# Two-layer transformer block on one core: three of the four GpSimd steps of a ternary weight piece move one slot each in the written order

## The chip, the cores and the metric

The kernel runs on one core of one Trainium2 chip. The core has a matrix engine (TensorE, PE in the profile), a vector engine (VectorE, DVE), a scalar engine (ScalarE, ACT), GpSimd (POOL) and a queue engine for transfers (SyncE, SP). Each engine has an instruction queue of its own, and the program ties the queues together by semaphores. The metric is the device time of one execution in microseconds (us); smaller is better. The runs of the kernel before took 1178.61, 1179.34 and 1179.58 us, median 1179.34 us.

## The reference

Two layers, each an attention and a feed-forward network on the same normalised input, added to the residual. What matters here is the attention of layer 0 (2 x 1024 tokens, 32 query heads of width 8, causal) and the weights of layer 1's feed-forward network, which the reference quantises to three values per group of 64 before it uses them:

```python
def ternary_quant(w_fp32, g=GROUP_SIZE):
    w = w_fp32.astype(jnp.bfloat16)
    w_g = w.reshape(-1, g)
    scale = jnp.clip(jnp.mean(jnp.abs(w_g), axis=-1, keepdims=True), 1e-08, None)
    q = jnp.clip(jnp.round(w_g / scale), -1, 1)
    w_hat = (q * scale).reshape(w.shape)
    return w + jax.lax.stop_gradient(w_hat - w)

x = x + _L0_attn_ref(xn, ...) + _L0_ffn_ref(xn, ...)
xn = _layernorm(x, axis=-1)
x = x + _L1_attn_ref(xn, ...) + _L1_ffn_ref(xn, ...)
```

The last line of `ternary_quant` is computed as it stands, (q * scale - w) + w in bfloat16, so a piece of weights ends in four elementwise steps: the sign from two comparisons, times the scale, minus w, plus w.

## The kernel before

**Layer 0's attention** (`attention0`) works in blocks of 128 queries, sixteen of them: the eight of batch 0 upwards, then the eight of batch 1 downwards. Two streams run side by side in it. One finds each row's largest score: `max_unit` has TensorE make scores in PSUM (L930 the causal mask, L958 the products) and VectorE reduce each 128x512 tile of them (L970); the score tiles come from a pool of three PSUM buffers, so TensorE can't run far ahead of VectorE. `take_max` closes a block's maxima, and they go through memory into the rows of the query tile. The other stream weighs: `weigh` makes transposed scores (L1022), ScalarE takes the exponentials (L1032), and where the key block is the query block itself (j == i) GpSimd clears what lies above the diagonal in each of them (the `affine_select`, L1036; called a select here). `gather` multiplies with the values (L1052), one key block later.

**The written order.** The text of the program is a chain of slots. `one_slot` writes some maxima (`advance`), then at most one piece of layer 0's feed-forward network (`pieces`, with its bfloat16 elementwise work on VectorE, L196 to L206 and L295 to L305, and `out_piece`, whose additions into the residual, L261, are on GpSimd), then calls `tick`. `tick` counts the slot and runs what `after(n, f)` had set down n slots before. Behind each `one_slot`, the main loop writes one `weigh`: two exponentials, and in a diagonal block two selects. So the four selects of a half block are written in two consecutive slots.

Only TensorE's queue is held to the written order (`manual_schedule(engines={PE})`). The queues of the other engines are laid out by the framework's planner when the program is built: it goes through a simulated time, and gives an engine that is free the earliest written instruction among those that are ready. `tc.issue_after(ins)` adds one condition: what the block writes for the engine of `ins` is queued behind `ins`. Here `ins` is `reduced`, the latest L970, so this holds VectorE's instructions and no others.

**The ternary weights** are made during layer 0 in twelve pieces of 128x512: eight of `w_gate_up`, into `wgu_bf`, four of `w_proj`, into `wp`, for use in layer 1. `ternary` is a generator. Its first step loads the piece by a DMA from GpSimd's queue (L326, two buffers `tw`), its second takes absolute values on VectorE (L329), and its third has TensorE sum the groups (L332), VectorE scale and compare (L334, L336, L337) and GpSimd do the four last steps, L338 to L341, each of which reads what the one before it wrote. They are called the four links here. `next_weights` is called when a block's maxima are done, from the fourth block on: it does the second step of one piece, sets `rest_of_weights` down for two slots later, and takes the first step (the load) of the next piece. `rest_of_weights` takes the third step. Nothing in layer 0 reads the finished weights: `wgu_bf` is first read behind the attention, when it is copied to float32 (L1294), `wp` by L667.

## Time and profile before

| what | number |
|---|---|
| median of three runs | 1179.34 us |
| the profiled execution | 1180.16 us, its span 1178.4 us |
| mean granted TensorE clock over the span | 0.936 |
| busy over the span | PE 88%, DVE 65%, ACT 46%, POOL 29% |
| busy from 90 to 790 us (layer 0's attention) | PE 607.89, DVE 571.12, ACT 428.42, POOL 244.05 us |
| one link on POOL (L338 to L341), 48 of them | 1.14 to 1.71 us |
| one select on POOL (L1036), 128 of them | 637 ns median |
| start of the twelve pieces' first link | 177.3, 225.0, 277.8, 352.5, 416.7, 480.3, 543.6, 602.1, 651.2, 687.0, 717.5, 736.4 us |

The profile is of one execution. [...] A timeline row gives start, length, engine, line and operation, the tiles written and read, and in brackets how long the engine had been idle before and whose result it waited for. The chain of waits is followed back from the last instruction to what released each step. TensorE's matmul ends are modelled.

### The profile page before, as it was taken

The page shows a single profiled execution, that of the slowest core. Times are in us where ns is not written, and L with a number is a line of the kernel's source. Part 1 is how long each engine was busy: PE and PEld are TensorE (multiplying, and loading weights), DVE is VectorE, ACT ScalarE, POOL GpSimd, SP SyncE. Part 2 cuts the span into 40 slices and gives each one's busy share as a digit, 9 for nine tenths or more (in the row PEclk, how much of TensorE's full clock was granted, in tenths as well). Part 3 has the DMA queues.
Part 4 walks back from the last instruction along what each step waited for, and adds up shares of the span by engine and source line. Part 5 has one row for each costly group of instructions (what it writes and reads, how often), then busy time and mean ns, then how long its engine had stood idle before and what let it go on. Part 6 is the DMA issues. An engine that isn't in the chain of part 4 may idle for free.

```text
span 1178.4 us, 19285 instructions
## 1 busy us (share of the span) xinstructions
PE 1039.2 (88%) x7446; PEld 497.8 (42%) x7462; DVE 764.8 (65%) x1448; ACT 545.2 (46%) x983; POOL 345.4 (29%) x394
## 2 busy tenths in 40 slices
PE   5758787897988989897989998989999999999998
PEld 2333331231432222232323333334566676676676
DVE  7467988889688997789896899334333433433331
ACT  2004461673456757586767777742232322322221
POOL 2007233324235121412223335564222312312200
PEclk9758896998899989998999999999899999999989
DMA  5342101101102010100000110019431431421200
GB/s 173 112 110 73 48 3 38 21 21 45 49 5 50 1 27 10 41 5 8 21 19 10 27 28 3 5 19 132 62 52 28 80 65 30 86 51 28 38 19 19
DMA packets 65859, 48.99 MB, mean 42 GB/s; under 512 B 20840, under 2 KB 59368, under 8 KB 65768
## 3 DMA queue, kind: packets, MB, share of 16 engines
q1 hardware_dynamic: 60568, 39.05, 15.4%
q0 software_dynamic: 4112, 8.26, 2.9%
q8 instruction: 58, 0.95, 0.3%
q10 hardware_dynamic: 1088, 0.46, 0.1%
q14 instruction: 33, 0.27, 0.1%
HBM read 34.12 MB, written 15.20 MB: 42 GB/s over the span
## 4 chain that ended last, share of the span: by engine, by line
PE 55%; DVE 27%; DMA 7%; ACT 4%; POOL 3%; issue 2%; SPq 1%; DVEq 0%; ACTq 0%; POOLq 0%
DVE mx L970 14%; PE f1gu L632 8%; PE acc L1052 8%; PE s L1022 6%; PE f1o L667 5%; PE m L958 3%; PE sk L524 3%; PE sq L489 3%; PE gu L288 2%; DMA qscr<-ptq 2%; PE pqk L440 2%; ACT p L1032 2%; PE m L930 1%; DMA qkv<-all 1%; SPq L882 1%
## 5 line engine op out<-in xcount | busy, mean ns | idle before, releaser
L970 DVE TENSOR_REDUCE mx<-m 128x1 f32<-128x512 f32 (+3 forms) x608 | 372.8, 654 | 91.4 <-PE m L958 55.2
L1032 ACT ACTIVATE p<-s 128x512 f32<-128x512 f32 x576 | 307.0, 604 | 133.7 <-PE s L1022 131.2
L1052 PE MATMUL acc<-p,v 128*9 128x512 f32 x1152 | 171.1, 613 | 2.4 <-ACT p L1032 1.2
L958 PE MATMUL m<-k,qmain 64*128 64x512 bf16 (+3 forms) x384 | 94.8, 357 | 50.5 <-DVE mx L970 39.2
L1036 POOL TENSOR_SCALAR_AFFINE_SELECT p<-p 128x512 f32<-128x512 f32 x128 | 84.8, 685 | 162.2 <-ACT p L1032 161.9
L632 PE MATMUL f1gu<-xnT,wgu 128*128 128x512 f32 x256 | 117.6, 603 | 3.1 <-DVE wgu L1294 3.1
L958 PE MATMUL m<-kmain,qmain 64*128 64x512 bf16 (+3 forms) x384 | 83.4, 333 | 24.9 <-DVE mx L970 23.0
L958 PEld LDWEIGHTS <-qmain 64*128 64x128 bf16 x768 | 50.3, 99 | 80.4 <-issue 51.2
L930 PEld LDWEIGHTS <-ident_h 64*128 64x128 bf16 x832 | 45.2, 97 | 88.1 <-issue 65.3
L646 POOL TENSOR_TENSOR sq<-h 128x512 f32<-128x512 f32 x28 | 29.2, 1041 | 180.0 <-DVE h L642 180.0
L930 PE MATMUL m<-mask_q,ident_h 64*128 64x128 bf16 (+3 forms) x832 | 75.2, 221 | 2.4 <-DVE mx L970 2.3
L1022 PE MATMUL s<-qmain,k 64*128 64x512 bf16 x288 | 67.8, 393 | 9.0 <-ACT ob L258 3.1
L632 PEld LDWEIGHTS f1gu<-xnT,wgu 128*128 128x128 f32 x256 | 47.5, 195 | 51.8 <-issue 47.8
L1022 PE MATMUL s<-qmain,kmain 64*128 64x512 bf16 x288 | 64.0, 389 | 4.9 <-ACT p L1032 2.3
L1022 PE MATMUL s<-qlast,k 35*128 35x512 bf16 x288 | 64.0, 390 | 0.0
L641 DVE SCALAR_TENSOR_TENSOR h<-h,f1gu 128x512 f32<-128x512 f32 x32 | 22.0, 687 | 64.5 <-ACT h L640 64.5
L1022 PEld LDWEIGHTS <-k 64*128 64x128 bf16 (+1 forms) x576 | 21.1, 95 | 97.9 <-issue 89.8
L497 DVE TENSOR_REDUCE m<-sq 128x16 f32<-128x2048 f32 x16 | 36.7, 2292 | 39.6 <-PE sq L489 38.9
L1022 PE MATMUL s<-qlast,klast 35*128 35x512 bf16 x288 | 61.1, 386 | 0.0
L667 PE MATMUL f1o<-k,h 128*128 128x256 f32 x256 | 59.4, 388 | 0.5 <-DVE on L557 0.5
L667 PEld LDWEIGHTS f1o<-k,h 128*128 128x128 f32 x256 | 48.9, 193 | 9.0 <-issue 1.7
L640 ACT ACTIVATE h<-f1gu 128x512 f32<-128x512 f32 x32 | 19.1, 597 | 65.7 <-PE f1gu L632 65.6
(274 smaller groups left out, 1597.6 us busy)
## 6 DMA issues: line engine op xcount, KB each, us to landing
qmain<-qscr SPq DMA_DIRECT2D x64, 96.0 KB
qkv<-all SPq DMA_DIRECT2D x16, 384.0 KB
qscr<-ptq POOLq DMA_DIRECT2D x6, 384.0 KB, 4.1
x<-in_x SPq DMA_DIRECT2D x16, 128.0 KB
qmain<-qscr SPq DMA_DIRECT2D x32, 64.0 KB
qs<-qkv SPq DMA_DIRECT2D x16, 128.0 KB
ks<-qkv SPq DMA_DIRECT2D x16, 128.0 KB
vs<-qkv SPq DMA_DIRECT2D x16, 128.0 KB
```

The lines of the kernel that those rows point to most:

```text
L489: nc.tensor.matmul(ps[:, s, r, :], columns(q, slice(S * s, S * s + HD + 8), 4 * b + r), columns(k, slice(S * s, S * s + HD + 8), 4 * b + r ...
L497: nc.vector.tensor_reduce(m, ps, AX.X, ALU.max, negate=True)
L524: nc.tensor.matmul(ps[:, s, r, :], columns(k, slice(S * s, S * s + HD + 9), 4 * b + r), columns(q, slice(S * s, S * s + HD + 9), 4 * b + r ...
L632: nc.tensor.matmul(ps[g], wgu[:, k, g * HID + hc * P : g * HID + (hc + 1) * P], xnT[n][:, k, :], start=(k == 0), stop=(k == 1),)
L667: nc.tensor.matmul(po, hs[hc // 2][:, hc % 2, i * P : (i + 1) * P], wp[:, hc, :], start=(hc == 0), stop=(hc == NHC - 1),)
L930: nc.tensor.matmul(out[e][:, :, lo:], ident_h[rows, t, :], rhs.to_broadcast([HALF, out[e].shape[1], P - lo]), start=start and t == 0, stop ...
L958: nc.tensor.matmul(sc[e][:, s * width : (s + 1) * width], qst[b, i][0][rows, p, :], kst[b][0][rows, lo // 512, p // 4, 0:width], start=not ...
L970: reduced = nc.vector.tensor_reduce(mx[b, i][:, part, e, pairs[0] : pairs[0] + n], sc[e][:, : n * width].rearrange("p (s k) -> p s k", s=n ...
L1022: nc.tensor.matmul(sc[e], kst[b][n][rows, j // 4, u, j % 4 * P : (j % 4 + 1) * P], qst[b, i][n][rows, 4 * u : 4 * u + 4, :], start=n == 0, ...
L1032: nc.scalar.activation(p, sc[e], AF.Exp, scale=scale)
L1036: nc.gpsimd.affine_select(out=by_head, in_=by_head, compare_op=ALU.is_ge, fill=0.0, base=0, pattern=[[0, 4], [1, P]], channel_multiplier=-1,)
L1052: nc.tensor.matmul(acc[32 * s : 32 * s + HD0 + 1, :], vst[b][:, j, 4 * G + s, :], ps[s], start=(j == 0), stop=(j == i),)
```

## The change

The four links are no longer written in one step of the generator: there is a `yield` behind each of the first three. `rest_of_weights` takes one step, and as long as the generator isn't exhausted it sets itself down again for the next slot. So the first link stays in the slot it was written in, and the second, third and fourth are written one, two and three slots later. 

```diff
         nc.gpsimd.tensor_tensor(m, m, lo, ALU.subtract)
+        yield
         nc.gpsimd.tensor_tensor(m, m, s, ALU.mult)
+        yield
         nc.gpsimd.tensor_tensor(m, m, w, ALU.subtract)
+        yield
         nc.gpsimd.tensor_tensor(dst, m, w, ALU.add)
...
             def rest_of_weights(u):
                 with tc.issue_after(reduced.ins):
-                    next(u, None)
+                    more = next(u, self_end)
+                if more is not self_end:
+                    after(1, lambda: rest_of_weights(u))
```

## The prediction

> **What bounds the kernel now.** I read the page first: busy shares, slices, then the chain that ended last.

> ```profile
> PE 1039.2 (88%) x7446; PEld 497.8 (42%) x7462; DVE 764.8 (65%) x1448; ACT 545.2 (46%) x983; POOL 345.4 (29%) x394
> ...
> POOL 2007233324235121412223335564222312312200
> ...
> PE 55%; DVE 27%; DMA 7%; ACT 4%; POOL 3%; issue 2%; SPq 1%; DVEq 0%; ACTq 0%; POOLq 0%
> ```

> GpSimd is busy 29% of the span and holds 3% of the chain. So the links' own duration (48 of about 1.2 us, some 57 us) isn't what ends late; they can only matter through whom they hold up. There are two candidates: the selects queued behind them, for which the value matmuls wait, and VectorE, which holds 27% of the chain.

> For the first I took the view of line L1036, the selects, and who waits for them:

> ```profile
> L1036 POOL TENSOR_SCALAR_AFFINE_SELECT p<-p x128: 627/637/1507, 97.4 to 777.1; 128x512 f32<-128x512 f32 x128
> ...
>   PEld acc L1052: 12.1, 19
>   ACT ob L257: 0.9, 1
>   ACT p L1032: 0.9, 1
>   PE acc L1052: 0.8, 2
> ```

> In the whole layer TensorE waits some 13 us for selects, in 21 waits of 0.6 us. I then took the waits in twelve windows of 12 to 18 us, one round each piece's links: no wait of TensorE for a select is in any of them. What a link does to a select costs TensorE nothing today.

> For the second I compared every VectorE instruction that overlaps a link with the short instructions of its own line. Eighteen are longer than usual, by 15.5 us in sum. One stands out. First GpSimd, then VectorE, in the timeline around piece 1:

> ```profile
> 177.29 1.14 POOL L338 TENSOR_TENSOR tmg<-tmg,tlg 128x512 bf16<-128x512 bf16 x1
> 178.40 0.63 POOL L1036 TENSOR_SCALAR_AFFINE_SELECT p<-p 128x512 f32<-128x512 f32 x1
> 179.00 1.14 POOL L339 TENSOR_TENSOR tmg<-tmg,tsg 128x512 bf16<-128x512 bf16 x1
> 180.10 0.63 POOL L1036 TENSOR_SCALAR_AFFINE_SELECT p<-p 128x512 f32<-128x512 f32 x1
> 180.71 1.14 POOL L340 TENSOR_TENSOR tmg<-tmg,twg 128x512 bf16<-128x512 bf16 x1
> 181.81 0.63 POOL L1036 TENSOR_SCALAR_AFFINE_SELECT p<-p 128x512 f32<-128x512 f32 x1
> 182.42 1.14 POOL L341 TENSOR_TENSOR wgu_bf<-tmg,twg 128x512 bf16<-128x512 bf16 x1
> 183.86 0.61 POOL L326 DMA_DIRECT2D twg<-in_w_gate_up  x1 [0.30 <-POOL wgu_bf L341]
> ```

> ```profile
> 179.14 4.70 DVE L302 TENSOR_SCALAR fw<-fw 128x1024 bf16<-128x1024 bf16 x1
> 183.76 0.68 DVE L970 TENSOR_REDUCE mx<-m 128x1 f32<-128x512 f32 x1
> ```

> L302 is usually 0.43 us long (its median of 16). Here it begins inside L339 and ends 0.28 us after L341, so it stood still until GpSimd stopped: 4.3 us. The chain of waits runs through it, and TensorE's next L958, at 184.50, waits 4.64 us for the reduce behind it. In this stretch VectorE sets the end, and GpSimd sets VectorE.

> The same view round piece 7 shows the other case. There the links follow one another with nothing between:

> ```profile
> 544.83 1.57 POOL L339 TENSOR_TENSOR tmg<-tmg,tsg 128x512 bf16<-128x512 bf16 x1
> 546.48 1.15 POOL L340 TENSOR_TENSOR tmg<-tmg,twg 128x512 bf16<-128x512 bf16 x1
> 547.71 1.15 POOL L341 TENSOR_TENSOR wgu_bf<-tmg,twg 128x512 bf16<-128x512 bf16 x1
> ```

> L340 ends at 547.63 and L341 starts at 547.71: a gap of 0.08 us between two links that depend on each other. VectorE gets in at each such gap: its four L178 between 545.31 and 549.34 take 1.24 to 1.31 us in place of 0.40, one link each. In piece 1 the rows overlap (179.00 + 1.14 is past 180.10): no gap, and VectorE is out for the whole run.

> [...]

> **The change, part by part.** It removes and adds no work: the same 48 links, 128 selects and loads. No wait is added, since each link already needs the one before. It moves three links of a piece one, two and three slots down the written order, on GpSimd's queue alone; TensorE's queue, VectorE's and SyncE's instructions are written as before. `issue_after` names a VectorE instruction, so it holds no link back.

> What does a later place do? GpSimd's queue isn't in written order. The load at 183.86 is the proof: it is written by the call whose first instruction, L329, runs at 217.29, and it went out 33 us ahead, as soon as its buffer was free. The planner takes what is ready; the written place decides only between instructions ready together. So:

> - Pieces 2, 6 to 11 and 12 (links at 225.0, 480.3 to 717.5, 736.4): the four links run one behind the other. Nothing else was ready between them, so a lower rank changes nothing: 0 us. The additions L261 behind pieces 6 and 12 come after the fourth link now, and I expect them there again.
> - Piece 4 (352.5): two L261 stand between links. They depend on each other as the links do, so the pairs go on alternating: 0 us.
> - Piece 1: the exponentials of all four selects were done by 177.25, so all were ready. Behind L338 a select goes (the next link isn't ready the moment the first ends); then L339, written earlier, goes before the third select; then again a select, then L340 before the fourth. With the change, L339 is written behind the first two selects and before the last two, L340 behind all four. I expect select, L338, select, L339, select, select, L340, L341. The run is as long as today, but L340 and L341 now meet, with the 0.08 us gap. VectorE's L302 gets in there: by the rows, 181.32 + 1.14 = 182.4 us, plus 0.28, is 182.7 in place of 183.84, **1.1 us earlier**. Bounds: two selects now meet too, at 181.3, and L302 may get in there (2.2 us earlier; the select pair at 326.97 let an L302 through at 0.68 us in all); or at neither, 0. I take 1.1, the row nearest to it being the links of piece 7.
> - Piece 3 (277.8 to 288.0): L341 stands before three selects now, and is written two slots behind the first of them then. I expect one more select before it. VectorE's L199 (285.03, 1.38 us in place of 0.41, on the chain) waits for L341 today. It would wait for a 0.6 us select and get in (0.5 us less) or for both (0.6 us more). I take 0.
> - Piece 5 (416.7): the last select and L341 may change places. VectorE does eight reduces in a row there (417.41 to 422.3), none of them lengthened: 0 us.

> The loads behind L341 (L326, issued from GpSimd's queue) move by well under 1 us. The next piece takes its data over 30 us later, so the time to the next piece hides that; gone only if links slid past the next piece's L329, which comes 8 us behind the fourth link even in the tightest case (722.8 to 731.2). The selects move up by about a link where they move at all, and cost TensorE nothing today.

> Sum: -1.1 us, with bounds of -2.7 (2.2 and 0.5) and +0.6. The profiled execution is 1180.16 us (span 1178.4 and 1.8 around it), 0.8 above the median of 1179.34. On the median: **1178.2 us**, -0.1%. Under 0.2%, 2.4 us, a measurement of this kernel can't tell from no change.

> **Rivals.**

> *It does nothing.* If the fourth select in the planner's time was not ready when L340 was, the order is today's everywhere: 1179.3. For it: the planner's times aren't the chip's. Against: 177.25 is 3.5 us ahead.

> *Faster: the links really come apart.* If selects that wait for ScalarE are put between links, GpSimd falls idle between them and VectorE's bfloat16 work goes through. The excess on the chain is then at stake: 4.28 (L302), 0.97 (L199 at 285), 2.66 (three L178 at 545), 0.88 (L296 at 605) and 0.84 (L299 at 654), 9.6 us in all. A link alone still holds a VectorE instruction up once, so about half is to be had: 1179.3 - 5 = 1174.3. Against: seven of the twelve runs have nothing near to put between.

> *Slower: more runs without a gap.* Links that alternate with independent work, each ready when the other ends, shut VectorE out for the whole run (4.3 us in piece 1, against 0.6 to 0.9 a gap). The places are piece 3, with four selects and VectorE's L196 and L199 ready from 283.76, and piece 6, with additions and selects to 497. In piece 3, shut out to 288.03 in place of 284.51: 3.5 us. It decides from the point where no two links and no two selects meet: one such run gives 1182.8, two 1186.3. Against: at 283.76 VectorE got in between a link and a select.

> **How the numbers follow.** Chances: the forecast 0.50 (its own range 1176.6 to 1179.9), nothing 0.22, faster rival 0.13, slower rival 0.15. The range takes in half of each outer rival, 1174.3 to 1182.8, and leaves 0.14 out. Faster by over 0.2% (under 1177.0): the rival's 0.13 and 0.01 from the forecast's edge; slower (over 1181.7): 0.15; the rest 0.71.

> **What would show it.** Right: piece 1's row order as above, L302 near 3.6 us or less, the other eleven pieces' links back to back or alternating as now. Wrong: links with idle time before them (faster rival), or another VectorE row of 3 us or more over a GpSimd run (slower rival), or TensorE waiting for selects in the twelve windows.

## The result, and the profile after

The changed kernel takes 1183.29 us (median of 20 runs, 1178.64 to 1189.59), the kernel before 1179.95 us in the same comparison (20 runs, 1176.74 to 1186.09). The ratio is 1.0031, with a 95% interval from 1.0016 to 1.0046: slower by 0.3%, 3.3 us between the medians. I had forecast 1178.2. The profiled execution took 1185.47 us, with a span of 1183.8 and a mean granted TensorE clock of 0.925 (before: 1180.16, 1178.4 and 0.936).

The lines stand one to four further down in the changed file: the links are L339, L341, L343 and L345, the selects L1040, the reduces of the maxima L974, their matmuls L962, the load L327. L196, L199 and L302 keep their numbers. First the page: busy times, GpSimd's slices and the chain by engine.

```profile
PE 1047.6 (88%) x7446; PEld 502.8 (42%) x7462; DVE 764.3 (65%) x1448; ACT 545.3 (46%) x983; POOL 343.6 (29%) x394
...
POOL 2007233314235121411223335554322312312200
...
PE 58%; DVE 26%; DMA 5%; ACT 4%; POOL 3%; issue 2%; SPq 1%; DVEq 0%; ACTq 0%; POOLq 0%
```

The page doesn't tell where 3.3 us went: the counts are equal, GpSimd has 1.8 us less, VectorE 0.5 us less, TensorE 8.4 us more, and TensorE's longer time goes with the lower clock (0.925 against 0.936). The selects' view, which I had used to rule out one way, still rules it out: TensorE waits for selects a little less than before (10.5 us in 18 waits, against 12.1 in 19).

```profile
L1040 POOL TENSOR_SCALAR_AFFINE_SELECT p<-p x128: 624/634/1172, 96.2 to 781.3; 128x512 f32<-128x512 f32 x128
...
  PEld acc L1056: 10.5, 18
```

Every engine's instructions stand in the order of before, but for two exchanges of neighbours on GpSimd: in piece 1 the last select now goes ahead of the third link, in piece 3 the second select goes ahead of the fourth link. These are the two that the prediction expected. Piece 1, the timeline of GpSimd, then of VectorE:

```profile
177.08 1.14 POOL L339 TENSOR_TENSOR tmg<-tmg,tlg 128x512 bf16<-128x512 bf16 x1
178.18 0.62 POOL L1040 TENSOR_SCALAR_AFFINE_SELECT p<-p 128x512 f32<-128x512 f32 x1
178.78 1.14 POOL L341 TENSOR_TENSOR tmg<-tmg,tsg 128x512 bf16<-128x512 bf16 x1
179.89 1.21 POOL L1040 TENSOR_SCALAR_AFFINE_SELECT p<-p 128x512 f32<-128x512 f32 x2
181.07 1.14 POOL L343 TENSOR_TENSOR tmg<-tmg,twg 128x512 bf16<-128x512 bf16 x1
182.29 1.21 POOL L345 TENSOR_TENSOR wgu_bf<-tmg,twg 128x512 bf16<-128x512 bf16 x1
```

```profile
178.93 3.58 DVE L302 TENSOR_SCALAR fw<-fw 128x1024 bf16<-128x1024 bf16 x1
182.42 0.68 DVE L974 TENSOR_REDUCE mx<-m 128x1 f32<-128x512 f32 x1
183.02 1.03 DVE L303 TENSOR_TENSOR fw<-fg,fw 128x1024 bf16<-128x1024 bf16 x1
```

This is the order written down in advance, and the length too: L302 takes 3.58 us instead of 4.70. It gets in at the 0.08 us gap between L343 (ends 182.21) and L345, and ends soon behind it. L303, the next two-byte row, now overlaps the fourth link and takes 1.03 us, where it took 0.67 before. Piece 7 is as it was, its links one behind the other.

Piece 3 is where it went the other way. GpSimd before has one select between the third and the fourth link (L340, L341):

```profile
283.05 1.16 POOL L340 TENSOR_TENSOR tmg<-tmg,twg 128x512 bf16<-128x512 bf16 x1
284.16 0.84 POOL L1036 TENSOR_SCALAR_AFFINE_SELECT p<-p 128x512 f32<-128x512 f32 x1
284.98 1.14 POOL L341 TENSOR_TENSOR wgu_bf<-tmg,twg 128x512 bf16<-128x512 bf16 x1
286.08 1.99 POOL L1036 TENSOR_SCALAR_AFFINE_SELECT p<-p 128x512 f32<-128x512 f32 x3
```

VectorE before, with its two rows of two-byte data at 0.75 and 1.38 us:

```profile
283.76 0.75 DVE L196 TENSOR_SCALAR fe<-fw 128x1024 uint16<-128x1024 uint16 x1
284.43 0.68 DVE L970 TENSOR_REDUCE mx<-m 128x1 f32<-128x512 f32 x1
285.03 1.38 DVE L199 TENSOR_SCALAR fe<-fe 128x1024 bf16<-128x1024 bf16 x1
```

VectorE after, then GpSimd after:

```profile
282.24 3.60 DVE L196 TENSOR_SCALAR fe<-fw 128x1024 uint16<-128x1024 uint16 x1
285.76 0.68 DVE L974 TENSOR_REDUCE mx<-m 128x1 f32<-128x512 f32 x1
286.36 0.41 DVE L199 TENSOR_SCALAR fe<-fe 128x1024 bf16<-128x1024 bf16 x1
```

```profile
281.53 1.16 POOL L343 TENSOR_TENSOR tmg<-tmg,twg 128x512 bf16<-128x512 bf16 x1
282.64 1.22 POOL L1040 TENSOR_SCALAR_AFFINE_SELECT p<-p 128x512 f32<-128x512 f32 x2
283.83 1.14 POOL L345 TENSOR_TENSOR wgu_bf<-tmg,twg 128x512 bf16<-128x512 bf16 x1
284.93 1.39 POOL L1040 TENSOR_SCALAR_AFFINE_SELECT p<-p 128x512 f32<-128x512 f32 x2
```

L196 comes 0.71 us after the third link's start, as before (283.76 against 283.05 there). Then it stands still through two selects, the fourth link and one more select: 2.85 us more than before. L199 behind it no longer waits, which gives 0.97 us back. The chain of waits, cut to this stretch, now holds L196 as one long piece, and TensorE, which has three score tiles to run ahead in, waits 3.75 us at 286.49:

```profile
282.32 3.52 DVE fe L196
285.84 0.60 DVE mx L974
286.44 0.33 DVE fe L199
```

```profile
286.49 0.58 PE L962 MATMUL m<-k,qmain 64*128 64x512 bf16 x1 [3.75 <-DVE mx L974]
```

Taken row by row against before, VectorE's work falls 1.9 us behind at piece 3 (2.85 less 0.97), after it had come 0.8 us ahead at piece 1 (the 1.12 us of L302 less the 0.36 of L303). That makes 1.1 us, and the medians differ by 3.3, so 2.2 us aren't in these rows. This execution is 5.3 us longer than the profiled one of before. It loses 3.3 us from 288 to 372 us (in the time of before), and 3.1 us more behind 1100 us, where no link runs. From 301.5 to 372 us TensorE is granted half its clock in three steps of 3.4 us, two of them from 306.5 to 313.3, one from 361.1 to 364.5, where before ran at the full clock all through. The view by windows, before and then after (the value ahead of the last two is the granted clock):

```profile
300.00:320.00 20.00, 19.08 (x140) 9.09 (x140) 11.19 (x26) 11.44 (x22) 5.36 (x4) 0.96 0.14 46
...
350.00:370.00 20.00, 17.34 (x93) 5.53 (x93) 15.09 (x25) 10.44 (x24) 14.03 (x18) 1.00 0.24 59
```

```profile
300.00:320.00 20.00, 19.30 (x121) 10.07 (x120) 10.50 (x23) 9.26 (x19) 5.35 (x4) 0.83 0.13 43
...
350.00:370.00 20.00, 16.54 (x91) 5.75 (x89) 14.92 (x23) 11.10 (x24) 14.99 (x19) 0.91 0.23 59
```

One profile can't tell whether these steps belong to the change, so they are a second question for the experiments.

### The profile page after: what moved, and what is told of

Read it like the earlier page. It is cut to its first block, busy times and chain, and to the rows that moved or that the text cites. A ratio compares the mean times of both kernels' runs of the same rounds, so it can differ in the third digit from the quotient of the medians.

```text
span 1183.8 us, 19285 instructions
## 1 busy us (share of the span) xinstructions
PE 1047.6 (88%) x7446; PEld 502.8 (42%) x7462; DVE 764.3 (65%) x1448; ACT 545.3 (46%) x983; POOL 343.6 (29%) x394
## 4 chain that ended last, share of the span: by engine, by line
PE 58%; DVE 26%; DMA 5%; ACT 4%; POOL 3%; issue 2%; SPq 1%; DVEq 0%; ACTq 0%; POOLq 0%
DVE mx L974 13%; PE f1gu L636 9%; PE acc L1056 8%; PE s L1026 7%; PE f1o L671 5%; PE m L962 3%; PE sk L528 3%; PE sq L493 3%; DMA qscr<-ptq 2%; PE gu L288 2%; PE pqk L444 2%; ACT p L1036 2%; PE m L934 1%; SPq L886 1%; PE acc L543 1%
## 5 line engine op out<-in xcount | busy, mean ns | idle before, releaser
L974 DVE TENSOR_REDUCE mx<-m 128x1 f32<-128x512 f32 (+3 forms) x608 | 372.4, 653 | 96.1 <-PE m L962 58.4
L1036 ACT ACTIVATE p<-s 128x512 f32<-128x512 f32 x576 | 306.8, 605 | 139.0 <-PE s L1026 136.4
L962 PE MATMUL m<-k,qmain 64*128 64x512 bf16 (+3 forms) x384 | 95.4, 365 | 50.2 <-DVE mx L974 38.4
L1040 POOL TENSOR_SCALAR_AFFINE_SELECT p<-p 128x512 f32<-128x512 f32 x128 | 83.3, 674 | 164.2 <-ACT p L1036 164.0
L962 PE MATMUL m<-kmain,qmain 64*128 64x512 bf16 (+3 forms) x384 | 83.5, 332 | 24.5 <-DVE mx L974 22.4
L962 PEld LDWEIGHTS <-qmain 64*128 64x128 bf16 x768 | 50.2, 100 | 83.1 <-issue 54.4
L671 PE MATMUL f1o<-k,h 128*128 128x256 f32 x256 | 62.5, 402 | 0.5 <-DVE on L561 0.5
```

Source lines behind the costliest of these rows:

```text
L671: nc.tensor.matmul(po, hs[hc // 2][:, hc % 2, i * P : (i + 1) * P], wp[:, hc, :], start=(hc == 0), stop=(hc == NHC - 1),)
L962: nc.tensor.matmul(sc[e][:, s * width : (s + 1) * width], qst[b, i][0][rows, p, :], kst[b][0][rows, lo // 512, p // 4, 0:width], start=not ...
L974: reduced = nc.vector.tensor_reduce(mx[b, i][:, part, e, pairs[0] : pairs[0] + n], sc[e][:, : n * width].rearrange("p (s k) -> p s k", s=n ...
L1036: nc.scalar.activation(p, sc[e], AF.Exp, scale=scale)
L1040: nc.gpsimd.affine_select(out=by_head, in_=by_head, compare_op=ALU.is_ge, fill=0.0, base=0, pattern=[[0, 4], [1, P]], channel_multiplier=-1,)
```

## The experiments

The first theory (A): the exchange in piece 1 gains 1.1 us, the exchange in piece 3 costs, through L196, and nothing else happens. Rivals: (B) the exchanges are worth nothing and the clock's steps made the difference; (C) piece 1 costs. All ratios are to the kernel before in the same comparison, with a 95% interval.

### One exchange at a time, and the change again

For one piece alone, each of the three new steps is bound to its name; `g00` is piece 1, `g02` is piece 3.

```diff
-        yield
+        if name == "g00":
+            yield
```

> The links are written apart in the first piece alone; on GpSimd's queue one pair is exchanged against the kernel before (the fourth select of the diagonal and the third link, near 181 us), and no other queue differs. Theory A, the lockout has moved from piece 1 to piece 3: the long L302 near 179 us falls from 4.7 to 3.6 us, the L196 near 284 us stays near 0.75 us, and the time is 1.1 to 1.3 us under the kernel before, ratio near 0.999. Theory B, the exchanges matter nothing and the difference is the phase of TensorE's clock steps: within 0.2% of before, either sign. Theory C, the exchange in piece 1 is what costs, since it shifts everything behind it against the clock steps: 2 us or more above the kernel before, ratio 1.002 or more.

> The links are written apart in the third piece alone; on GpSimd's queue one pair is exchanged against the kernel before (the second select of the diagonal and the fourth link, near 285 us), and no other queue differs. Theory A: L196 near 284 us grows from 0.75 to about 3.6 us, TensorE waits near 3.7 us for the reduce behind it, and the time is 2 to 5 us above the kernel before: 1.7 us directly (2.7 lost, 1.0 given back because L199 no longer waits) and the rest by TensorE's clock, granted at half for one or two steps of 3.4 us more in the 30 us behind it. Ratio 1.002 to 1.004. Theory B: within 0.2% of before. Theory C: no slower than before.

> The changed kernel once more, beside the others on the same chip. Theory A: between the two single exchanges, their sum: 1 to 4 us above the kernel before, ratio 1.001 to 1.0035; its profile shows L302 near 3.6 and L196 near 3.6 us again, the same as in the first profile of it. Theory B: the two long rows come at other places or with other lengths than in the first profile, and the ratio is nearer to 1 than 1.002. Theory C: the ratio of the kernel with the first piece alone.

Measured: piece 1 alone 0.9983 (0.9962 to 1.0004), piece 3 alone 1.0028 (1.0007 to 1.0049), the changed kernel again 1.0025 (1.0003 to 1.0047). The rows follow the edit exactly. With piece 1's exchange L302 takes 3.58 us and piece 3 is that of before; with piece 3's, L302 takes 4.70 and L196 3.60. VectorE's rows in piece 3, first with the exchange of piece 1 alone, then with that of piece 3 alone:

```profile
281.19 0.75 DVE L196 TENSOR_SCALAR fe<-fw 128x1024 uint16<-128x1024 uint16 x1
282.46 1.37 DVE L199 TENSOR_SCALAR fe<-fe 128x1024 bf16<-128x1024 bf16 x1
```

```profile
283.50 3.60 DVE L196 TENSOR_SCALAR fe<-fw 128x1024 uint16<-128x1024 uint16 x1
```

So the wait belongs to the order of GpSimd's instructions and not to chance: it comes out within 0.02 us in the profiled executions of the same order (L302 3.58 us each time, L196 3.60, 3.60 and 3.61). C falls. Since the intervals were wide, both were run once more:

> The exchange of piece 1 alone, once more, because its ratio (0.9983, from 0.9962 to 1.0004) and that of the kernel with the extra instruction in piece 3 (1.0004) don't sit well together. If L302's 1.1 us (4.70 to 3.58) comes through to the end, 0.998 to 0.9995; if it is given back, 0.9995 to 1.001.

> The exchange of piece 3 alone, once more: if the wait of L196 (3.60 us instead of 0.75, less the 0.97 us that L199 no longer waits) is all that costs, a ratio near 1.0016; if the whole first wait counts, 1.0023; the first reading was 1.0028, from 1.0007 to 1.0049.

Measured: piece 1 alone 1.0000 (0.9975 to 1.0026), piece 3 alone 1.0050 (1.0027 to 1.0073). The first lies where its text says that the gain is given back, the second is above all that its text allowed. By the two readings piece 1 is worth 0 to 2 us, in which the 0.8 us of its rows lies, but that they reach the end isn't shown. Piece 3 costs some 3.3 to 5.9 us, over the 1.9 us that its own rows lose (the first interval takes 1.9 in, the second doesn't). B falls as the whole answer, but a part of the loss isn't in the rows of piece 3.

### Opening the run again: one small instruction more

If order alone does it, another order must undo it, even with more work. To the changed kernel one GpSimd instruction was added, in piece 3 only. It reads two columns of what the third link wrote and nobody uses its result.

```diff
         nc.gpsimd.tensor_tensor(m, m, w, ALU.subtract)
+        if name == "g02":
+            gt = pool.tile([P, 2], BF, tag="gt", name=f"gt3{name}", bufs=1)
+            nc.gpsimd.tensor_tensor(gt, m[:, 0:2], m[:, 0:2], ALU.add)
         yield
```

> The kernel after, with one more GpSimd instruction of 128x2 elements in piece 3 alone: it reads what the third link wrote, and comes in GpSimd's order behind the first of the two selects that now meet, so that these two lie apart again, with an instruction between them that waits for the link. Theory A (VectorE is let in behind a link only where an instruction that waits for that link stands two places further on, as the fourth link did in the kernel before): L196 in piece 3 takes 0.7 to 1.2 us instead of 3.60, and the time is that of the exchange in piece 1 alone, a ratio of 0.998 to 1.000. Rival (VectorE simply waits until the selects are through, and the added instruction makes that later): L196 takes 3.6 to 3.8 us and the ratio stays at 1.002 to 1.004.

GpSimd's timeline of this kernel (links L343 and L348, the small instruction L346, selects L1043), then VectorE's:

```profile
281.30 1.17 POOL L343 TENSOR_TENSOR tmg<-tmg,twg 128x512 bf16<-128x512 bf16 x1
282.40 0.84 POOL L1043 TENSOR_SCALAR_AFFINE_SELECT p<-p 128x512 f32<-128x512 f32 x1
283.23 0.18 POOL L346 TENSOR_TENSOR gt3g<-tmg 128x2 bf16<-128x2 bf16 x1
283.37 0.80 POOL L1043 TENSOR_SCALAR_AFFINE_SELECT p<-p 128x512 f32<-128x512 f32 x1
284.15 1.14 POOL L348 TENSOR_TENSOR wgu_bf<-tmg,twg 128x512 bf16<-128x512 bf16 x1
```

```profile
282.00 0.75 DVE L196 TENSOR_SCALAR fe<-fw 128x1024 uint16<-128x1024 uint16 x1
283.28 0.41 DVE L199 TENSOR_SCALAR fe<-fe 128x1024 bf16<-128x1024 bf16 x1
```

L196 is back at 0.75 us, and each select that let VectorE in is 0.2 us longer (0.84 and 0.80 instead of 0.62). The ratio is 1.0004 (0.9993 to 1.0016), just above the 0.998 to 1.000 that was expected. One instruction more on GpSimd made the kernel 0.27% faster (1.0031 to 1.0004), 3.2 us, where the rows differ by the 2.85 us of L196 alone. (The two ratios are of different comparisons; in this one the changed kernel with TensorE filled, below, had 1.0036.) So the wait of L196 does reach the end. But the rows of this kernel should put it ahead of before: 0.8 us in piece 1 and 0.97 in piece 3. It comes out 0.5 us behind, so some 2.2 us are lost without that wait too, the same remainder as in the changed kernel.

The same in all twelve pieces, behind the second and third links (24 small instructions, the same two lines without the condition):

> The kernel after, with such an instruction of 128x2 elements behind the second and behind the third link of all twelve pieces, 24 in all. Theory A: in pieces 1 and 3 no VectorE row waits over 2.5 us any more (L302 3.58 and L196 3.60 now), the ratio to the kernel before is 0.996 to 0.999. Rival (what counts is GpSimd's time, and 24 more instructions add to it): rows of VectorE stay long or move to other pieces, ratio 1.002 to 1.005.

Measured 1.0025 (1.0012 to 1.0037): theory A missed, in the number and in both rows. L302 in piece 1 took 3.74 us. The rival's number was met, but not its cause: against the changed kernel (1.0031) the 24 instructions added nothing. In piece 3 the added instructions changed the order again, and L196 now came during a select, before the third link, and was shut out for 4.50 us. GpSimd (small instructions L343 and L347, links L345 and L349, selects L1044), then VectorE:

```profile
280.53 0.65 POOL L1044 TENSOR_SCALAR_AFFINE_SELECT p<-p 128x512 f32<-128x512 f32 x1
281.14 1.15 POOL L345 TENSOR_TENSOR tmg<-tmg,twg 128x512 bf16<-128x512 bf16 x1
282.25 0.63 POOL L1044 TENSOR_SCALAR_AFFINE_SELECT p<-p 128x512 f32<-128x512 f32 x1
282.85 0.18 POOL L347 TENSOR_TENSOR gt3g<-tmg 128x2 bf16<-128x2 bf16 x1
283.00 1.14 POOL L349 TENSOR_TENSOR wgu_bf<-tmg,twg 128x512 bf16<-128x512 bf16 x1
284.10 1.21 POOL L1044 TENSOR_SCALAR_AFFINE_SELECT p<-p 128x512 f32<-128x512 f32 x2
```

```profile
281.09 4.50 DVE L196 TENSOR_SCALAR fe<-fw 128x1024 uint16<-128x1024 uint16 x1
```

This also refutes the rule by which I had placed the small instruction, that a waiter two places behind a link lets VectorE in behind that link: here link, select and waiter stand just as in the kernel above, and VectorE, which had come earlier, was not let in at 282.29. Nor is such a waiter needed, as the expectation had it: in the kernel before, L199 was let in between the fourth link and three selects (it ends at 286.41).

### Filling TensorE's idle time

> The kernel after, with eight matmuls of 128x512 elements that nobody reads put into TensorE's queue where it stands idle for 3.75 us while VectorE waits in piece 3. L196 stays at 3.60 us by every theory. If the rest of the loss (about half of the 3.3 us, beyond the 1.7 us of the wait itself) comes from the lower TensorE clock that the idle time sets off, the stretch from 300 to 320 us has the granted clock of the kernel before (0.93 and 1.00) and the ratio falls to 1.0005 to 1.0015. If the clock's steps fall as they like, the ratio stays at 1.002 to 1.004.

```diff
-                wait_busy({0: 55, 4 + 1: 10}.get(at, 0))
+                wait_busy({0: 55, 4 + 1: 10, 101: 8}.get(at, 0))
```

Measured 1.0036 (1.0023 to 1.0049), with L196 at 3.62 us. In this execution the clock from 300 to 320 us was 1.00, but two half steps came between 350 and 370 (0.83 in each ten of them). The eight matmuls took 1.90 us from 276.95 on, and TensorE still stood idle for 2.20 us behind them. So in this execution filling half of TensorE's idle time didn't undo the lower clock (the two 0.83); the changed kernel run again, with nothing filled in, had the same 1.00 and the same two steps. What filling all of it would do isn't shown.

Whether the steps belong to the change can be read from all profiled executions. From 288 to 372 us those without an exchange in piece 3 lost next to nothing against before: piece 1 alone 0.1 and 0.1 us, the two kernels of the next section with only pieces 1 or 1 and 3 moved 0.1 and -0.2. Those with an exchange in piece 3 lost 3.3 and 2.2 (the changed kernel twice), 2.2 (filled), 1.6 and 0.4 (piece 3 alone), 3.3 (one small instruction) and 2.7 us (24 of them), in half-clock steps worth about 1.4 us each, less 0.7 to 1.4 us that each had gained up to 300 us (the 1.4 us is an estimate: these losses and gains together, over the number of steps). The two with links moved in more pieces, and one such step each, lost 0.4 and 0.5. So in this stretch the steps go with the exchange in piece 3, and the kernel with one small instruction has them without the wait. Behind 1100 us they don't: there the kernel of the next section with all pieces moved lost 3.9 us. The size fits the remainder of 2.2 us of the changed kernel and of the one with a small instruction, but not piece 3 alone in its second reading, where 4.0 us are left and its one profile lost 0.4 here. The mean clock of all runs points the same way for the changed kernel (0.933 twice, against 0.936) and for piece 3 alone (0.934 and 0.932). It doesn't for the filled one and the one with 24 small instructions, which had 0.936 and were slower than before too. That the clock is the whole remainder is therefore argued and not shown, and what in the exchange sets the steps off stays open.

### The links behind the selects

If VectorE gets in between links that follow one another, a piece's links should all come behind the block's selects. In the kernel before, `affine_select`'s result is kept in `select[0]`, and the links are written four slots later and queued on GpSimd behind that select:

```diff
+        if name == "g00":
+            yield
         nc.gpsimd.tensor_tensor(m, m, lo, ALU.subtract)
...
                 with tc.issue_after(reduced.ins):
-                    next(u, None)
+                    more = next(u, self_end)
+                if more is not self_end:
+                    after(4, lambda: links(u))
+
+            def links(u):
+                with tc.issue_after(select[0].ins):
+                    next(u, None)
```

For all pieces the condition is left out, for pieces 1 and 3 it names both, and for all but the twelfth it is `name != "p3"`.

> All four links of a piece stay together, and are held on GpSimd's queue behind the last select written before them, four slots later than VectorE's part. No select stands between links. Theory A: no run of alternating links and selects is left in pieces 1, 3 and 5, VectorE gets in at the gaps between links (0.08 us each), L302 near 179 us is 0.9 to 2 us long and L196 and L199 near 284 us under 1.5 us each, so the time is 1 to 4 us under the kernel before, ratio 0.997 to 0.999. Theory B: within 0.2% of before. Theory C says nothing of this kernel.

> The kernel before, with the four links of piece 1 alone put behind the block's last select; all other pieces as before. Theory A: the selects come first, the links then wait for each other one by one, L302 takes about 1.3 us instead of 4.70, nothing in piece 3 changes (L196 0.75), so some 3.4 us go and the ratio is 0.996 to 0.998. Rival (the earlier kernel with all pieces behind the selects gained nothing because a shorter wait in piece 1 is given back at once): L302 short too, but the ratio is 0.9990 to 1.001.

> The kernel before, with the four links of pieces 1 and 3 behind the last select of their blocks, all others as before. Theory A: piece 1 brings the 3.3 us that it brought alone (ratio 0.9972), and in piece 3 L199 waits about 0.8 us instead of 1.38, so 0.9964 to 0.9974. Rival (in piece 3 the later links make the next piece's load late, and a new wait comes in): 0.998 to 1.000.

> The kernel before, with the links of all pieces but the twelfth behind a select. The kernel with all twelve had a ratio of 1.001, and its VectorE rows near 745 us, at the twelfth piece, came some 3 us late. If that piece gave the gain back, this one comes out at 0.996 to 0.998; if the gain is lost in other pieces or by the clock, 0.999 to 1.001.

| links behind the selects in | ratio (95% interval) | L302, piece 1 | L196 and L199, piece 3 |
|---|---|---|---|
| all pieces | 1.0010 (0.9984 to 1.0036) | 1.34 | 0.75, 0.77 |
| piece 1 | 0.9972 (0.9959 to 0.9985) | 1.34 | 0.75, 1.37 |
| pieces 1 and 3 | 0.9969 (0.9946 to 0.9991) | 1.34 | 0.75, 0.77 |
| all but the twelfth | 0.9994 (0.9972 to 1.0017) | 1.35 | 0.75, 0.77 |

Piece 1 alone comes out where its text said, 3.3 us (0.28%) faster than the kernel before: 1176.31 us against 1179.93. Its rows fit: 4.70 to 1.34 is 3.4 us, of which L303 and L305 behind it, now beside links (1.03 and 1.06 us in place of 0.67 and 0.68), give 0.7 back; the interval reaches from 1.8 to 4.8 us. Pieces 1 and 3 together came out as expected too. GpSimd and VectorE there, with links L340 to L343 and selects L1039:

```profile
175.28 2.81 POOL L1039 TENSOR_SCALAR_AFFINE_SELECT p<-p 128x512 f32<-128x512 f32 x4
178.06 1.14 POOL L340 TENSOR_TENSOR tmg<-tmg,tlg 128x512 bf16<-128x512 bf16 x1
179.28 1.22 POOL L341 TENSOR_TENSOR tmg<-tmg,tsg 128x512 bf16<-128x512 bf16 x1
```

```profile
178.15 1.34 DVE L302 TENSOR_SCALAR fw<-fw 128x1024 bf16<-128x1024 bf16 x1
```

L302 now waits for one link and enters at the gap of 0.08 us behind it (179.20 to 179.28; L302 ends at 179.49). With all pieces the expected gain wasn't there, though the rows in pieces 1 and 3 were as expected. In the twelfth piece the links came among the additions L261, and the small VectorE rows that close a block's maxima took 1.19 and 1.07 us instead of 0.18 each, and VectorE's rows fell 6.0 us behind between 741 and 748 us, of which 2.3 came back. Yet without the twelfth piece the gain was still not there (0.9994, where 0.996 to 0.998 would have put the blame on that piece), though its interval reaches down to 0.9972. Whether one of pieces 2 and 4 to 11 gives it back, or the clock, is open. In this one profile VectorE's rows lose 2.4 us between 225 and 250 us, at a granted clock of 0.74 from 220 to 230 us (before: 0.99); the kernel with all pieces moved has the same order there and loses nothing.

## Why the prediction was wrong

- **GpSimd's own share and the selects** cost nothing: right (the chain's 3% is unchanged, and TensorE waits 10.5 us for selects, not more).
- **The planner's rule** (ready instructions in written order): right for all twelve pieces. There were two exchanges, each where it was expected, and "it does nothing" and "the links really come apart" fell with that.
- **Piece 1**, "1.1 us earlier": right in order and mechanism, and in the size of L302 (4.70 to 3.58). Its lower bound, that L302 might get in where two selects meet, wasn't met. The sum left out L303 behind it, which gives 0.36 back, so the rows gain 0.8 us.
- **Piece 3**, "I take 0": this is the step that failed. The order was foreseen ("one more select before it"), but I priced only L199, which then waited for the fourth link, and left L196 out as a row that had got in at 0.75 us and would do so again. L199 did gain 0.97 us; L196 lost 2.85. The sum for piece 3 is +1.9 us, outside its bounds of -0.5 and +0.6.
- **The slower rival** had the place, the mechanism and the rows right (piece 3, VectorE shut out; priced at 3.5 us, and 2.85 measured). Two things in it were wrong. Its condition, "no two links and no two selects meet": two pairs of selects meet in piece 3, and VectorE was not let in between the first pair. And its "against", that at 283.76 VectorE had got in between a link and a select: I took one observation of one order for a property of the place. With two readings from the same page pointing in opposite directions (let in at 284.2, shut out at 180.1, both at a link followed by a ready select), the boundary was unknown, and the chance of 0.15 was too small.
- **The wait through a whole run of GpSimd's instructions**, read from one row (4.3 us, L302): right. L196 waited 3.60 us through four instructions in the changed kernel, and 4.50 through six in the one with 24 small instructions. One row of piece 7 was misread: of the four L178 near 545 us three took 1.24 to 1.31 us, the fourth 0.40; the later sum counts three.
- **The size**: 1.9 less 0.8 is 1.1 us; the other 2.2 of the 3.3 us had no term in my sum at all. By the profiled executions TensorE's half-clock steps behind piece 3 are the likely place, which isn't shown; I had taken the clock as given.

## What to carry to other kernels

Before a GpSimd instruction is moved, list the VectorE rows that overlap its neighbours (not those of two-byte data alone: the float32 L178 took 1.24 to 1.31 us in place of 0.40 beside links), and price the longest run without a gap for each of them, also for those that get through today. What lets VectorE in reliably in these runs is a GpSimd instruction that needs the result of the one just before it (a gap of 0.08 us), so dependent steps are best kept next to each other, with independent work ahead of the group or behind it. Make such a move only where a row shows a wait: in one piece it gave 0.28%, in two 0.31%, in all twelve nothing.
